# A two-block transformer kernel on one core: the expert layers' tokens scattered to expert regions, expert weights kept in SBUF, and the middle of the kernel put in a written order

## The chip, the core and the metric

The kernel runs on one core of a Trainium2 chip. The metric is the device time of one execution in microseconds; the median of 3 runs of the kernel before is 853.11 us (852.16 to 854.4). All arithmetic is in fp32. PE is the matmul engine (PEld its weight load), DVE the vector engine, ACT the activation engine, POOL the general engine, which also issues the indirect DMAs, and SP the engine that issues the plain DMAs.

## The reference, cut to what matters

The input x has 16 sequences of 128 tokens with 128 features. Every layer adds to x what it computes from a normalized x:

```python
x = x + xcond(ln(x), cond, ctx)       # self-attention, cross-attention to ctx, GLU feed-forward
x = x + ffn0(ln(x))                   # shared gated expert + 7 routed gated experts, top 2
x = x + slots(cond, ctx, ln(x))       # 3 turns of slot attention over ctx
x = x + ffn1(ln(x))                   # 8 routed experts (relu), top 1
```

The two expert layers, which the change is about:

```python
def expert(h, g, u, d):               # g, u: 352 x 128, d: 128 x 352
    return einsum('...i,hi->...h', silu(h @ g.T) * (h @ u.T), d)
# ffn0: 2048 tokens
out = expert(x, sg, su, sd)           # shared, for every token
probs = softmax(x @ wr.T + rb); scores, idx = top_k(probs, 2); scores /= scores.sum()
out += sum over the 2 chosen e of scores[e] * expert(x, rg[e], ru[e], rd[e])
# ffn1: 2048 tokens
p = softmax(x @ w_gate + b_gate); e = argmax(p)
out = (relu(x @ W1[e] + b1[e]) @ W2[e] + b2[e]) * max(p)    # W1: 128 x 512, W2: 512 x 128
```

## The kernel before, in words

Tokens lie 128 to a batch on the partitions; r (128 x 16 x 128) holds the running sum of all 16 batches. After attention the work is done in four groups of four batches (512 tokens).

The order of work is set in two ways. The two attention phases stand in a `manual_schedule` block (lines 798 to 802): each engine gets its instructions in the order in which the code issues them. All the rest is put in order by the framework's scheduler, by priority (the order of the code) and its own estimate of when things are ready; on the chip each engine then works through its queue in order.

1. Loads on SP (lines 114 to 131), self-attention and cross-attention (to about 408 us). The softmax shares of cross-attention go into tiles "es" with four buffers (line 459).
2. GLU feed-forward: `glu_norm` and `glu_prologue` normalize a group on DVE, transpose it on PE and scale it on DVE (line 544). `glu_body` takes four columns, each of two 128x512 matmuls, a Gelu on ACT and a product on DVE, and then the output matmuls. `wide` tiles in PSUM have three buffers.
3. First expert layer. `moe0_route` normalizes a group (`Routed.normed`, scaled on DVE by `scale_shift`, line 230), computes the routing logits, marks the two best experts (`one_hot_max`, called twice), and writes tokens and weight to a table `tok` in DRAM. When all groups are routed, `Routed.sort` gives each token-expert pair a place in a list sorted by expert (line 940 on), inverts that list by masks on DVE and small matmuls on PE (lines 983 to 1009), and so finds for each tile of 128 places which rows to fetch (`frm`) and where results go (`to`). `moe0_shared` computes the shared expert for each group. `silu_gate` writes silu as a Tanh on ACT and two scalar_tensor_tensor steps on DVE.
4. `Routed.tiles` runs the 38 tiles (lists of different experts don't share a tile, hence 38 for 4096 pairs). Per tile: `fetch` gathers 128 rows by an indirect DMA on POOL (line 1054); `weights` reads the expert's row into a register on SP and loads 576 KB of weights from DRAM (line 1044, six buffers); a transpose, 6 up-matmuls, the gate, 3 down-matmuls, a scale on ACT (line 1173), and an indirect DMA on POOL that scatters the results to `res0` in DRAM (line 1075). `combine` reads `res0` back and adds.
5. `slot_prologue` prepares the slot layer's weights and `slot_context` its keys and values from ctx; it adds a row to all 16 rows of "cb" on one partition, on POOL (line 1232). `slot_turns` runs the 3 turns, the groups one step apart.
6. Second expert layer: `moe1_route`, `sort`, and 23 tiles, as before with one expert per token. The sort of this layer also issues matmuls that compute nothing needed (`busy`, line 975).

The steps that the code itself does not name: `ln_stats` takes statistics by bn_stats on DVE, and the root by a `pow` on POOL (line 177); `t_tag(g)` are four PSUM tiles, one for each group; `value_load` (line 1041) is a register load.

## Time and profile before

| | us |
|---|---|
| median of 3 runs | 853.11 |
| the profiled execution, its own time | 857.12 |
| its span, first to last instruction | 855.4 |
| attention ends (last "ya" on PE) | 407.8 |
| first up-matmul of the first expert tiles | 502.75 |
| last scale of a first-layer tile | 590.9 |
| last r of the slot turns | 772.6 |
| last up-matmuls of the second layer's tiles begin | 847.9 |

The busy totals and the 40 slices of the page, each slice 21.4 us:

```profile
PE 783.4 (92%) x5415; PEld 615.5 (72%) x5415; DVE 575.8 (67%) x1820; ACT 431.7 (50%) x940; POOL 350.5 (41%) x440
...
PE   6999999999999999999899889989858989995987
...
PEclk9999999999999999999999989999889979985899
DMA  8200000001100000000200169974100000003893
```

A digit is a tenth of the slice in which the engine was busy; PEclk is the granted clock in tenths of full speed; DMA is the mean busy share of 16 DMA engines. The two stretches with a DMA digit of 9 are the tiles of the two expert layers. The rows that cost most on the engines which the change touches (count, then busy us and mean ns, then idle time before them):

```profile
L1158 PE MATMUL gum<-zTnm,wm 128*128 128x128 f32 x456 | 63.6, 282 | 0.0
L1054 POOL DMA_INDIRECT zsm<-tok,frmm x38 | 36.8, 968 | 32.5 <-DVE secm L1032 21.2
L1075 POOL DMA_INDIRECT res<-ysm,tom x38 | 37.3, 982 | 17.5 <-ACT ysm L1173 9.0
L1135 DVE SCALAR_TENSOR_TENSOR gsm<-thm,gum 128x384 f32<-128x384 f32 x38 | 21.1, 554 | 26.8 <-ACT thm L1133 26.1
```

In names of tiles the layer's letter is appended: m for the first expert layer, n for the second. An fp32 matmul shows as two records, so the 456 of the first row are 228 matmuls: six for each of 38 tiles. Since records of matmuls overlap, the rate of PE is read from the chain of work, where 12 such passes take 1.34 us.

### The profile page before, as it was taken

The numbers are of one execution on the slowest core, as the hardware profiler recorded it, in microseconds if no ns is written. First come the engines' busy times: TensorE is split into PE (matmuls) and PEld (weight loads), VectorE is DVE, ScalarE is ACT, GpSimd is POOL, SyncE is SP. The second block draws the span as 40 slices with busy tenths as digits, with TensorE's granted clock in tenths as the row PEclk, the third lists the DMA queues.
The fourth block names the chain that finished last, engine by engine and source line by source line (L and its number), as shares of the span: only waits on it lengthen the run. The fifth ranks groups of instructions, "written<-read, shape, count | busy, mean of one in ns | idle before, by whom it ended". The sixth has DMA issues, their size and how long they took to land.

```text
span 855.4 us, 15453 instructions
## 1 busy us (share of the span) xinstructions
PE 783.4 (92%) x5415; PEld 615.5 (72%) x5415; DVE 575.8 (67%) x1820; ACT 431.7 (50%) x940; POOL 350.5 (41%) x440
## 2 busy tenths in 40 slices
PE   6999999999999999999899889989858989995987
PEld 4688888877788777776656579988446756664876
DVE  3677768665856777797788946554477758867444
ACT  3567667676654554445122124434467757851332
POOL 2234233323233333436522077773443324432776
PEclk9999999999999999999999989999889979985899
DMA  8200000001100000000200169974100000003893
GB/s 312 98 2 1 2 1 2 1 2 41 38 25 11 11 11 11 11 11 1 79 26 26 59 217 324 334 261 143 51 1 2 1 1 1 13 25 117 312 333 132
DMA packets 36528, 65.18 MB, mean 76 GB/s; under 512 B 4578, under 2 KB 25013, under 8 KB 35811
## 3 DMA queue, kind: packets, MB, share of 16 engines
q1 hardware_dynamic: 32179, 55.11, 19.2%
q0 software_dynamic: 4272, 9.09, 3.4%
q8 instruction: 43, 0.70, 0.3%
q14 instruction: 34, 0.28, 0.1%
HBM read 55.71 MB, written 8.93 MB: 76 GB/s over the span
## 4 chain that ended last, share of the span: by engine, by line
PE 64%; DVE 15%; DMA 8%; POOL 5%; issue 3%; ACT 3%; SPq 0%; POOLq 0%; ACTq 0%; DVEq 0%
PE pq L325 6%; PE gum L1158 4%; PE pk L335 4%; PE te L482 4%; PE po L492 4%; PE s L429 4%; PE s L420 3%; PE ya L524 3%; PE pv L342 3%; PE pv L358 3%; PE ya L515 3%; DMA zsm<-tok,frmm 2%; PE ynm L1169 2%; DMA res<-ysm,tom 2%; PE glu L838 2%
## 5 line engine op out<-in xcount | busy, mean ns | idle before, releaser
L467 POOL TENSOR_TENSOR e<-e,ri 128x1024 f32<-128x1024 f32 x32 | 61.1, 1909 | 143.5 <-DVE ri L453 130.4
L440 DVE TENSOR_REDUCE mx<-s 128x8 f32<-128x1024 f32 (+1 forms) x64 | 64.4, 1006 | 63.2 <-PE s L429 47.7
L452 DVE TENSOR_REDUCE ri<-e 128x8 f32<-128x1024 f32 (+1 forms) x64 | 63.7, 995 | 18.9 <-ACT e L448 18.2
L461 POOL TENSOR_TENSOR es<-e,ri 128x512 f32<-128x512 f32 x64 | 43.4, 706 | 67.0 <-DVE ri L453 32.5
L325 PE MATMUL pq<-ha,wa 128*128 128x256 f32 x256 | 67.1, 398 | 2.7 <-ACT q L326 1.7
L445 DVE TENSOR_TENSOR e<-s,mx 128x1024 f32<-128x1024 f32 (+1 forms) x64 | 63.8, 997 | 2.0
L1158 PE MATMUL gum<-zTnm,wm 128*128 128x128 f32 x456 | 63.6, 282 | 0.0
L448 ACT ACTIVATE e<-e 128x1024 f32<-128x1024 f32 (+1 forms) x64 | 57.1, 892 | 5.9 <-DVE e L445 4.0
L1158 PEld LDWEIGHTS gum<-zTnm,wm 128*128 128x128 f32 x456 | 59.2, 199 | 0.1
L325 PEld LDWEIGHTS pq<-ha,wa 128*128 128x128 f32 x256 | 46.7, 199 | 10.4 <-ACT q L326 3.1
L1054 POOL DMA_INDIRECT zsm<-tok,frmm x38 | 36.8, 968 | 32.5 <-DVE secm L1032 21.2
L1075 POOL DMA_INDIRECT res<-ysm,tom x38 | 37.3, 982 | 17.5 <-ACT ysm L1173 9.0
L335 PE MATMUL pk<-ctxT,wa 128*128 128x154 f32 x256 | 40.5, 295 | 0.6 <-ACT k L336 0.6
L482 PE MATMUL te<-ident,e 128*128 128x128 f32 x256 | 39.6, 277 | 0.0
L482 PEld LDWEIGHTS te<-ident,e 128*128 128x128 f32 x256 | 30.5, 141 | 12.1 <-issue 8.7
L1135 DVE SCALAR_TENSOR_TENSOR gsm<-thm,gum 128x384 f32<-128x384 f32 x38 | 21.1, 554 | 26.8 <-ACT thm L1133 26.1
L429 PEld LDWEIGHTS s<-k,q 64*128 64x128 f32 x512 | 31.4, 190 | 10.4 <-issue 9.6
L483 ACT COPY eT<-te 128x512 f32<-128x512 f32 x64 | 37.8, 591 | 0.0
L496 ACT COPY oT<-po 128x512 f32<-128x512 f32 x32 | 18.5, 578 | 36.0 <-PE po L492 36.0
L420 PE MATMUL s<-k,ha 128*128 128x308 f32 x128 | 36.1, 423 | 0.0
L429 PE MATMUL s<-k,q 64*128 64x128 f32 x512 | 34.5, 281 | 1.8 <-DVE e L445 1.8
L335 PEld LDWEIGHTS pk<-ctxT,wa 128*128 128x128 f32 x256 | 35.1, 190 | 1.0 <-ACT k L336 0.9
(410 smaller groups left out, 2035.6 us busy)
## 6 DMA issues: line engine op xcount, KB each, us to landing
wm<-in_moe_w_dram SPq DMA_DIRECT2D x38, 576.0 KB
wn<-in_moe_w_dram SPq DMA_DIRECT2D x23, 578.0 KB
wa<-in_attn_w_dram SPq DMA_DIRECT2D x4, 1024.0 KB
ygm<-res SPq DMA_DIRECT2D x8, 256.0 KB
vor<-vo SPq DMA_DIRECT2D x16, 104.0 KB
vr<-vor SPq DMA_DIRECT2D x8, 208.0 KB
tok<-stm SPq DMA_DIRECT2D x4, 258.0 KB
tok<-stn SPq DMA_DIRECT2D x4, 258.0 KB
```

Of the source, the lines that this page charges most:

```text
L325: PE.matmul(pq[:, j, :], lhsT=wqk[:, w : w + P], rhs=hT, start=True, stop=True)
L335: PE.matmul(pq[:, j, :], lhsT=wqk[:, w : w + D], rhs=kvT, start=True, stop=True)
L420: PE.matmul(ps[:, par, : 4 * nk].rearrange("p (j k) -> p j k", k=nk), lhsT=st["qT"][:, i * P : (i + 1) * P], rhs=st["kT"][:, h0 : h0 + 4, ...
L429: PE.matmul(ps[:, par, j * nk : (j + 1) * nk], lhsT=st["qT"][h0 : h0 + DH, c, i * P : (i + 1) * P], rhs=st["kT"][h0 : h0 + DH, c, i * nk : ...
L440: V.tensor_reduce(self.mx, self.ps, AX.X, ALU.max)
L445: V.tensor_tensor(self.e, self.ps, self.mx.unsqueeze(3).to_broadcast([P, 2, 4, nk]), ALU.subtract)
L448: S.activation(self.e, self.e, AF.Exp, scale=1.0 / math.sqrt(DH))
L452: V.tensor_reduce(self.ri, self.e, AX.X, ALU.add)
L461: G.tensor_tensor(t[:, 8 * k0 : 8 * k1].rearrange("p (h k) -> p h k", h=8), e[:, :, k0:k1], ri.to_broadcast([P, 8, k1 - k0]), ALU.mult,)
L467: G.tensor_tensor(self.e, self.e, self.ri.unsqueeze(3).to_broadcast([P, 2, 4, self.nk]), ALU.mult)
L482: PE.transpose(t[:nk, j, :], e[:, par, j, :], ident)
L1158: PE.matmul(ps[j][:, c * P : (c + 1) * P], lhsT=w[:, k : k + P], rhs=zT, start=True, stop=True)
```

## The change

- **Scatter in place of sort and gather.** DRAM holds for each expert a region of 2048 rows (`disp`), filled once at the start with empty rows whose last word says that they belong to no token. As soon as a group is routed, `rank` counts its tokens' places in their experts' regions, and `send` scatters each batch by an indirect DMA on POOL, once for each of the two choices: 32 scatters in the first layer, 16 in the second. Each row carries features, weight and, as its last word, where its result goes. `plan` only finds where each tile starts. A tile's rows are then one plain DMA on SP (`fetch`, register load on SP, 8 buffers, 6 ahead), and its result is scattered by the row numbers in the tile itself, with empty rows dropped.
- **Weights kept in SBUF.** `load` brings all experts' weights into one tile (`wall`) by 7 or 8 DMAs. `weights` copies a tile's part from there, at an offset in a register: 768 or 516 columns on DVE, 384 or 640 on ACT, three buffers each.
- **Norms on ACT.** `act_scale` takes the place of `normalize` and `scale_shift` for GLU groups 2 and 3, the routed groups, and the contexts; the scaling of `hg` is on ACT too for those GLU groups.
- **Silu as one step.** ACT computes Silu, and DVE one product.
- **Written order.** From the GLU of group 1 to the loads of the second layer's weights, and around the second layer's tiles, a `manual_schedule` block gives the order. The slot prologue's pieces are dealt out over the tiles, one to a tile from the fifth on. Down-matmuls follow two tiles behind, transposes go two tiles ahead.
- "cb" lies on four partitions, so that its row addition is 128x512; "es" has three buffers; the `busy` matmuls of the sort are gone with it.

The core of the diff:

```diff
+    def dispatch(nm, ne, nt, pairs, w, k):
+        rows_ = -(-(ne * NTOK + (nt * P - pairs)) // (P * 4)) * P * 4
+        t = dram.tile([rows_, w], F32, name=f"disp{nm}")
...
+        V.memset(pad[:, :, w - 1 :].bitcast(I32), NONE)
+        n = rows_ // (P * k)
+        dma(
+            out=t.rearrange("(p n k) w -> p n (k w)", n=n, k=k),
+            in_=pad.rearrange("p k w -> p (k w)").unsqueeze(1).to_broadcast([P, n, k * w]),
+        )
...
-                t = self.ap_.tile([P, 8 * NC], F32, name=f"es{self.nm}", tag="es", bufs=4)
+                t = self.ap_.tile([P, 8 * NC], F32, name=f"es{self.nm}", tag="es", bufs=3)
...
+    def act_scale(z, src, rs, nmr):
+        for i in range(4):
+            S.activation(z[:, i, :], src[:, i, :], AF.Identity, bias=nmr[:, i : i + 1], scale=rs[:, i : i + 1])
...
+        def turned(self, i):
+            z = self.st[i][:, 0, :, :D]
+            t = transpose_n(z, P, 4, f"{self.nm}{i}", i)
+            self.zT[i] = rt.tile([P, 512], F32, name=f"zT{self.nm}{i}", tag="zT", bufs=4)
+            S.copy(self.zT[i], t.rearrange("p a b -> p (a b)"))
+            S.copy(self.st[i][:, 1, :, :D], z)
...
+        def rank(self, i):
...
+            PE.matmul(pr, lhsT=before, rhs=self.any[:, gs, :], start=True, stop=False)
+            PE.matmul(pr, lhsT=ones, rhs=self.cum[:, gs, :], start=False, stop=True)
...
+        def send(self, i):
+            for b in range(4):
+                for k in range(self.nk):
+                    G.indirect_dma_start(
+                        out=self.sent[(4 * i + b) * self.nk + k],
+                        out_offset=bass.IndirectOffsetOnAxis(ap=self.to[i][:, k, b : b + 1], axis=0),
+                        in_=self.st[i][:, k, b, :], in_offset=None,
+                    )
...
+        def address(self, part):
+            j = len(self.ws[part])
+            if j < self.nt:
+                self.at[part] = (V, S)[part].value_load(
+                    self.row[0:1, j : j + 1], min_val=0, max_val=(self.ne - 1) * self.wn
+                )
+
+        def weights(self, part):
...
+            (V.tensor_copy, S.copy)[part](w, self.wall[:, bass.ds(self.at[part] + part * self.up, n)])
+            self.ws[part].append(w)
+            self.address(part)
+
+        def fetch(self):
...
+            z = rt.tile([P, 2 * D + 2], F32, name=f"zs{self.nm}{j}", tag="zs", bufs=ZBUFS)[:, : self.width]
+            row = nc.sync.value_load(self.first[0:1, j : j + 1], min_val=0, max_val=self.disp.shape[0] - P)
+            dma(out=z, in_=self.disp[bass.ds(row, P), :])
...
             def finish(j):
...
+                down(self.ws[1][j], acts[j], y, ys, zs[j])
+                self.weights(1)
                 G.indirect_dma_start(
+                    out=wrote[j],
+                    out_offset=bass.IndirectOffsetOnAxis(ap=zs[j][:, self.width - 1 :].bitcast(I32), axis=0),
+                    in_=ys, in_offset=None, bounds_check=dst.shape[0] - 1, oob_is_err=False,
                 )
+                self.fetch()
...
+            for j in range(nt + 2):
+                if j + 2 < nt:
+                    turn(j + 2)
+                if j < nt:
+                    acts[j] = up(self.ws[0][j], zT[j], f"{self.nm}{j}", j)
+                    self.weights(0)
+                if j >= 2:
+                    finish(j - 2)
+                if j >= 4 and extras:
+                    extras.pop(0)()
...
     def silu_gate(a, gate, up, nm, n):
-        S.activation(th, gate, AF.Tanh, scale=0.5)
...
-        V.scalar_tensor_tensor(gs, th, 1.0, gate, ALU.add, ALU.mult)
-        V.scalar_tensor_tensor(a, gs, 0.5, up, ALU.mult, ALU.mult)
+        S.activation(gs, gate, AF.Silu)
+        V.tensor_tensor(a, gs, up, ALU.mult)
...
+    with tc.manual_schedule():
+        m0.stats(0)
+        glu_stats(2)
+        glu_c(1, 0)
+        m0.scale(0)
+        glu_c(1, 1)
+        m0.turned(0)
+        glu_c(1, 2)
+        route_first(m0, 0)
+        glu_z(2)
+        glu_c(1, 3)
+        glu_in(2)
+        glu_residual(2)
+        route_second(m0, 0)
+        glu_c(2, 0)
+        glu_y(1)
+        m0.stats(1)
+        glu_stats(3)
+        m0.send(0)
...
+        shared_steps((0, 1), (0, 2))
+        m0.scale(3)
+        shared_steps((1, 0))
+        m0.turned(3)
+        shared_steps((0, 3))
+        route_first(m0, 3)
+        shared_steps((1, 1))
+        route_second(m0, 3)
+        m0.send(3)
+        shared_steps((1, 2))
+        m0.plan()
+        shared_steps((2, 0), (1, 3), (2, 1), (2, 2), (3, 0), (2, 3), (3, 1), (3, 2), (3, 3))
+        m0.tiles(moe0_up, moe0_down, slot_prologue())
+        for g in range(4):
+            m0.results(g)
+        for g in range(4):
+            if g > 1:
+                m0.combine(g - 2)
+            slot_context(g)
+        for g in (2, 3):
+            m0.combine(g)
+        m1.load()
+    slot_turns(range(4), lambda g: m0.sum[g])
...
     for g in range(4):
         moe1_route(m1, g)
-    m1.sort()
-    m1.tiles(moe1_up, moe1_down)
+    for g in range(4):
+        m1.send(g)
+    m1.plan()
+    with tc.manual_schedule():
+        m1.tiles(moe1_up, moe1_down)
```

`plan` also issues the first three register loads and copies of each part, and the first six fetches. In the written order, groups 1 and 2 follow the pattern of group 0, with the columns of the next GLU group or of the shared expert between the steps of the routing.

## The prediction, made before the change was run

> **What bounds the kernel now.** I read the busy time in stretches that I cut at the stages, because the page's shares average stages with different limits (columns: busy us and instruction count of PE, PEld, DVE, ACT, POOL; granted clock; DMA share; GB/s).
> ```profile
> 412.00:450.00 38.00, 34.16 (x165) 21.62 (x165) 33.33 (x141) 9.86 (x17) 17.04 (x34) 1.00 0.18 59
> 450.00:475.00 25.00, 24.29 (x122) 15.58 (x121) 20.98 (x93) 5.71 (x12) 3.84 (x10) 1.00 0.07 22
> 475.00:502.00 27.00, 21.51 (x116) 14.26 (x115) 20.60 (x81) 2.77 (x6) 9.60 (x10) 0.86 0.45 154
> 502.00:592.00 90.00, 86.28 (x734) 85.02 (x733) 50.09 (x116) 39.04 (x116) 64.00 (x67) 0.96 0.77 260
> 612.00:757.00 145.00, 120.05 (x675) 89.17 (x676) 107.53 (x542) 103.97 (x268) 58.47 (x100) 0.91 0.02 5
> 757.00:794.00 37.00, 27.29 (x122) 20.02 (x120) 23.45 (x153) 8.75 (x22) 9.26 (x17) 0.60 0.28 82
> 794.00:856.00 62.00, 52.32 (x390) 47.88 (x390) 28.71 (x92) 20.39 (x69) 42.84 (x44) 0.94 0.75 264
> ```
> PE is busy in 502 to 592 and nearly so in 412 to 475; 475 to 502 and 757 to 794 are the sorts, where it starves and the clock sags (0.86, 0.60). The chain in order of time says what stands there.
> ```profile
> 419.88 5.26 DVE stm L230 x4
> ...
> 489.66 1.23 POOL zsm L1054
> ...
> 493.70 6.31 DMA zsm<-tok,frmm
> ...
> 531.79 5.01 DMA zsm<-tok,frmm
> ...
> 539.49 4.95 DMA res<-ysm,tom
> ```
> From 463.8 to 489.5 it is DVE alone (sort, L1007 masks, silu), then gathers; inside the tiles only a patch at 531 to 566 is DMA. The 419.88 line is explained by the instructions of that window:
> ```profile
> 419.80 4.49 POOL L1232 TENSOR_TENSOR cb<-cb,brow 1x2048 f32<-1x2048 f32 x1
> 419.88 5.01 DVE L230 TENSOR_SCALAR stm<-r,ym,mvm 128x128 f32<-128x128 f32 x3 [1.04 <-POOL mvm L201]
> ```
> A norm of 0.26 us sat through a 4.5 us POOL operation.
>
> **Part by part.** Durations are of the profiled execution: span 855.4, own time 857.1, 4.0 above the median of 853.1. I sum differences and take them off the median.
>
> *Start and attention: 0 (-1 to +3).* The fills write 15,360 rows of 520 B and 17,408 of 1,032 B, 26 MB; at the 260 GB/s of the tile stretch, 100 us, queued on SP behind the loads at 16 us. Cover: that queue's next user, the stores of L404, starts at 199.5. The memsets on DVE (0.1 to 0.3 us) precede the first x at 2.9. Three "es" buffers: the transposes that free one (L503, 347.3) lead the write into it (L461, 352.1) by 4.8 us, so nothing.
>
> *Middle, 411.4 (last yg of group 0) to the first tile at 502.* PE work by the chain: GLU columns 12 x 1.72 us (two matmuls of 0.86) = 20.7, GLU outputs 3 x 3.6, transposes 4.7, router 3.5, ranks 2, shared columns 12 x 1.72 = 20.7, shared outputs 4 x 2.6: 73. Removed from DVE: scale (L230, 9.4), zgl and hg of two groups (5), context norms (4.9), one of two silu steps (12 x 0.68), the masks of the sort (12): it falls from 75 to about 42 us, ranks included. ACT rises from 18 to some 40. POOL gets 32 scatters; a DMA_INDIRECT lasts 0.94 and they come 1.25 apart (L1054), 40 us, plus six norms of 1.8 and residuals, under 60 in all. None exceeds PE, so what costs is the written order: an in-order engine that waits holds what is behind it. Walking it: scale(0) needs the norm chain (0.7 add, 0.9 stats, 0.5, POOL 1.4, ACT 1.7 = 5.2 us), and the GELUs behind it on ACT hold their PSUM: PE waits about 1.9 us; rank(0) waits 2.1 for DVE's one-hots; z(3) and hg(3) cost 3; rank(3) 1.3: 8.3. The plan puts three register loads and three copies each on DVE and ACT; ACT's first load waits for the row that DVE works out (some 3 us of 0.17 us steps), and the silu of shared column (2,0) is queued behind it: 6 us, of which PE has 4.5 to do (two matmuls, an output): 1.5. With 1.5 for table loads (below), the tiles start at 411.4 + 73 + 11.3 = 495.7: -6.5 (-13 to 0). The last sends begin at some 474, end 10 us later, land by 486.5, the first fetch by 489: under shared work. SP's waits for the sends hold later fetches alone, and those PE needs only from 495.
>
> Silu may need another table than Tanh. The trace of before shows Gelu, Tanh, Gelu (430.86, 431.57, 432.64) with no load between; a load lasts 1.28 (L670) and the next ACTIVATE follows at once. Written order changes Silu/Tanh five times: 0 to 6.4 us of ACT. The Trainium skill (ScalarE: Activation LUTs, "What ACT_TABLE_LOAD costs") says a switch is 1.28 plus a drain of 1.38: 13 us. By the row, a quarter of 6.4 reaches PE, as three PSUM tiles run ahead: 1.5; by the rule 3. I take the row.
>
> *First tiles, 38.* PE's part is unchanged: 12 passes up twice 0.67, 0.67 down, 0.11 turn = 2.12 us. Gone: 22 MB of weight loads and 38 gathers, with the 8 us patch. New per tile on DVE: a copy of 768 columns; 128x208 took 0.256 (L392) and 128x32 0.166, hence 0.54; plus a product of 0.55 in place of two. On ACT: copy 384 (0.48, between 0.27 for 128 and 0.59 for 512), silu 0.50, turn 0.27, scale 0.37 = 1.6. Both also load a register: on SP that takes 0.27 + 0.15 + 0.02 = 0.44 (L1041); hidden behind their own copies, or else DVE is 1.55 and ACT 2.05, just below 2.12. POOL falls from two DMAs to one, 1.25. Here a rule speaks against the change: the skill (SBUF — State Buffer, the "DVE blocks DMA" trap) says an fp32 copy in SBUF locks POOL out of writing descriptors. The trace shows the lock between compute (4.5 us above), but three norms of that kind ran at 500.22 in 0.85 us beside a gather of 0.94, its usual time. By the row, scatters cost 1.25; by the rule 1.25 + 0.54 = 1.8, still covered. Steps total 38 x 2.12 - 1.3 (no down in the first two) + 1.4 (the last two) = 80.7; the prologue's sixteen pieces add 3 of PE and four norms of 1.6 on ACT, stalls of 2. That is 86 us against 88.1 (first up 502.75, last scale 590.9): -2 (-6 to +8).
>
> *Hand-over: -1.5 (-5 to +2).* Before, 13 us from the last scale to slot start. Still there: last scatter (at least 2.2 to land), reads, combine. Contexts 0 and 1, about 4.5 each in order, fill the wait: 11.5.
>
> *Slots: +1 (-2 to +4).* Same instructions; contexts 2 and 3 now run into the first turns.
>
> *Last layer: +3 (-5 to +9).* Before, from the last r at 772.6: first tile 794.2, steady from 800.3, last up at 847.9. The sort's twelve us on DVE go. But sixteen scatters x 1.25 = 20 us enter POOL's queue. Before, group 0's one-hot came only at 769.1 and its weight at 772.6 (L1388, L1399), at the end of the slots, so I let the sends start at 773, with two POOL norms of 1.5 between: 796; landing 2.4, fetch 2.4, turn: 801.5. Behind these sends nothing waits on POOL but those norms; PE waits for all of it, and the busy matmuls that kept it warm are gone. 23 tiles at 2.17 follow: DVE has copy 0.41, two relus 0.6, two sums 0.63, ACT 1.7, register load 0.44 each: tight, +1. The 4 us stall at 818 to 833 goes. Up(22) then comes at 849.3 plus 1, before 847.9, and the two late downs add half a microsecond: +3. If groups 0 to 2 send during the slots: -5.
>
> Sum: -6.5 - 2 - 1.5 + 1 + 3 = -6. 857.1 becomes 851; on the median **847**.
>
> **Rivals.**
> *Everything overlaps (832).* Middle stalls 5 instead of 11 (-6), no tile stalls (-2), early sends in the last layer (-7, part of their 8): 847 - 15. For it: POOL was 9.3 busy of 37 there; against: low-priority route steps came late before.
>
> *No change (853).* The last layer's queue and ACT's register loads eat the gain: first tiles at 2.2 (+3), last layer at its +6 (+3): 847 + 6. For: ACT at 2.05 of 2.12; against: register loads have copies to hide behind.
>
> *Slower (868): the ring of eight fetched tiles.* A buffer is refilled only when its tile's scatter, which reads its row numbers, has landed. From turn to end of down is 10.6 us (five steps), then scale 0.5, POOL 0.2, scatter, fetch: 11.4 + both landings, for eight tiles of 17.0. It decides from landings of 5.6 together. The page shows scatters 2.2 least, 4.6 median; gathers 2.4 and 5.2. At the least, 16.0: free. At the medians, 21.2, 2.65 per tile: +20 and +11, less some 10 of stalls counted above that fall into the same waits: 847 + 21. Against: those medians were beside weight loads of 260 GB/s that go; a tile now moves 130 KB in 2.1 us.
>
> That the change doesn't do what it says can't be: the loads, scatters and copies are instructions.
>
> **How the numbers follow.** A measurement here tells 0.3% (2.6 us) from nothing. Likeliest (847; own range 840 to 852) 0.47; overlap 0.22; no change 0.14; ring 0.17. Of the first, 0.04 lies above 850.5: faster 0.65, same 0.17, slower 0.18. The range goes from 830, below the overlap case, to 860, part of the way to the ring.
>
> **What would show it.** First up-matmul of the tiles near 496 (before 502.75), PE clock 1.0 throughout; masks and gathers absent; a step of 2.12 between turns, ACT under 2.1; table loads on ACT where Silu meets Tanh; the wait before the fetch on SP names the scatter if the ring binds; POOL's sends in a row from 773 to 796 in the last layer with PE idle and a low clock behind. I am wrong if attention stretches under the fills, if the written order stalls PE over 15 us, or if the slots change length.

## The result, and the profile after

The changed kernel takes 902.17 us (900.47 to 903.9, four runs) beside 853.75 for the kernel before in the same rounds: 1.0569 times as long (95% interval 1.0537 to 1.0601). The forecast was 847, a little faster. The profiled execution took 903.62 at a span of 901.9 and a mean clock of 0.935 (before: 857.12, 855.4, 0.951).

The page after, to set beside the busy totals and the 40 slices of before (a slice is now 22.5 us):

```profile
PE 784.0 (87%) x5367; PEld 613.4 (68%) x5367; DVE 550.1 (61%) x1700; ACT 481.5 (53%) x1058; POOL 335.3 (37%) x430
...
PEclk9999999999999999998988999799969899975998
DMA  8999700001200000006000111023500000003220
```

PE is busy for as long as before, to 0.6 us; the two stretches of DMA 9 in the tiles are gone, as they should be, and the fills stand in slices 2 to 4, where they cost nothing: group 0's output matmuls begin at 407.4 (before 407.6). DVE has 26 us less, ACT 50 more. So the 46.5 us by which the span grew are time in which PE waits. Busy time by stage, after (columns: stretch, its length, busy us and count of PE, PEld, DVE, ACT, POOL, granted clock, DMA share, GB/s):

```profile
411.40:520.70 109.30, 84.79 (x361) 52.81 (x360) 54.24 (x209) 35.16 (x74) 46.77 (x65) 0.88 0.21 71
520.70:621.00 100.30, 88.91 (x743) 87.50 (x744) 45.16 (x115) 57.38 (x166) 44.49 (x55) 0.95 0.15 43
621.00:800.10 179.10, 154.01 (x819) 108.87 (x817) 124.06 (x624) 116.85 (x295) 67.58 (x116) 0.90 0.11 39
800.10:831.00 30.90, 7.26 (x30) 5.93 (x30) 11.97 (x88) 8.07 (x18) 19.22 (x22) 0.52 0.25 86
831.00:884.80 53.80, 46.47 (x357) 43.26 (x357) 32.55 (x102) 29.48 (x84) 18.32 (x19) 0.96 0.23 65
884.80:901.90 17.10, 4.22 (x34) 3.70 (x32) 3.19 (x10) 1.30 (x4) 4.29 (x5) 0.76 0.03 9
```

Three stages of before, cut at the same events (the middle, the gated tiles, the last layer's first to last up-matmul):

```profile
411.40:502.60 91.20, 81.16 (x401) 51.95 (x400) 76.10 (x316) 19.06 (x35) 31.36 (x54) 0.96 0.23 76
502.60:590.90 88.30, 85.12 (x730) 84.24 (x728) 49.38 (x112) 38.26 (x114) 63.12 (x65) 0.97 0.78 264
794.20:847.10 52.90, 49.09 (x366) 45.02 (x366) 26.17 (x84) 19.63 (x66) 39.40 (x40) 0.96 0.88 307
```

The events that cut the stages are the first up-matmul of the gated tiles, the last scale, the end of the last r of the slots, and the first and last up-matmul of the second layer. The forecast counts from the times of the chain (502.75 and 847.9 in the table of before); the timeline has these two matmuls at 502.6 and 847.1. In us:

| stage | before | after | difference | forecast |
|---|---|---|---|---|
| attention, to 411.4 | 411.4 | 411.4 | 0 | 0 |
| middle | 91.2 | 109.3 | +18.1 | -6.5 |
| 38 gated tiles | 88.3 | 100.3 | +12.0 | -2 |
| hand-over and slots | 181.7 | 179.1 | -2.6 | -0.5 |
| head of the last layer | 21.6 | 30.9 | +9.3 | +7 |
| its first to last up | 52.9 | 53.8 | +0.9 | -5 |
| its end | 8.3 | 17.1 | +8.8 | +0.5 |

**The middle.** PE is busy 84.8 us and idle 24.5. In the stretches at half clock it is busy 23.7 us. If all of that work ran at half speed, half of it, 11.8, is the clock's loss, and 84.8 less 11.8 leaves 73.0, the work that was forecast. The waits before each rank and the half clock behind them are what was missing. The longest, in the timeline of after (start, us, engine, line, in brackets the idle time before and what ended it):

```profile
486.44 0.96 POOL L1006 DMA_INDIRECT dispm<-stm,tom  x1 [0.30 <-issue]
...
488.84 0.17 DVE L962 COPY stn<-idx 128x4 int32<-128x4 int32 x1 [7.93 <-DMA dispm<-stm,tom]
...
488.92 0.68 DVE L1192 TENSOR_TENSOR r<-ym,r 128x512 f32<-128x512 f32 x1
...
492.95 0.60 PE L991 MATMUL rankm<-anym,before 128*128 128x28 f32 x2 [7.17 <-DVE anym L1161]
```

The copy of row numbers at 488.84 belongs to the *second* expert layer. It stands outside the written block; the scheduler had room for it early and put it into DVE's queue, and as the staging buffers of both layers share a tag of three, it waits for the last scatter of gated group 2 to land. DVE works in order: r, the one-hots and rank(3) stand behind it. What such a wait does to PE's clock shows when the stretch around it is cut:

```profile
485.80:490.80 5.00, 0.00 (x0) 0.00 (x0) 1.79 (x9) 0.00 (x0) 1.29 (x2) 1.00 0.08 27
490.80:497.60 6.80, 4.65 (x10) 2.58 (x10) 3.47 (x19) 0.80 (x2) 1.91 (x2) 0.50 0.03 10
497.60:502.30 4.70, 4.70 (x32) 3.74 (x31) 3.83 (x22) 0.00 (x0) 3.50 (x4) 1.00 0.18 58
```

Of the other five waits of 2.25 us or more in this stage, four have 3.4 or 6.8 us at 0.50 behind them; the fifth, 2.68 us at the plan, does not. The changes of the clock lie on a grid of 3.41 us, and in this stage they go with how busy PE was in one such window. Two windows that the half clock follows, and the two that share the plan's wait:

```profile
412.30:415.71 3.41, 1.16 (x3) 0.14 (x1) 3.07 (x17) 0.88 (x3) 2.50 (x7) 1.00 0.73 209
470.33:473.74 3.41, 1.40 (x6) 1.01 (x7) 2.77 (x16) 0.20 (x1) 0.00 (x0) 1.00 0.03 11
501.05:504.46 3.41, 2.14 (x14) 1.31 (x12) 1.69 (x6) 1.02 (x2) 2.50 (x4) 1.00 0.12 39
504.46:507.87 3.41, 2.00 (x5) 1.04 (x6) 2.19 (x5) 1.60 (x3) 0.70 (x1) 1.00 0.15 44
```

The Trainium skill (TensorE: Matmul & The Clock Gate, "Part 1: The HAM clock gate") says that the clock is halved after an idle window of about 3.4 us, the window running free. The length and the grid agree with this trace. The idle window need not be whole here: PE was busy 1.16 and 1.40 us of the two that the half clock follows, and 2.00 and 2.14 us left it at 1.00 (ends of matmuls are modelled, so these figures are near ones).

**The gated tiles.** They run at 2.12 us each, as forecast, except from 557 to 583, where the four context norms stand among them:

```profile
564.18 0.86 DVE L203 BATCH_NORM_STATS2 stc<-ctxn 77x6 f32<-77x128 f32 x4
...
565.70 1.04 POOL L193 TENSOR_TENSOR yc<-qqc,mhalf 77x4 f32<-77x4 f32 x1
566.82 0.20 POOL L217 TENSOR_TENSOR mvc<-mvc,yc 77x4 f32<-77x4 f32 x1
567.05 1.65 ACT L868 ACTIVATE ctxn<-ctxn,mvc,yc 77x128 f32<-77x128 f32 x4 [3.27 <-POOL mvc L217]
568.60 0.24 ACT L1099 COPY zTnm<-tnm 128x128 f32<-128x128 f32 x1
568.75 0.48 ACT L1173 ACTIVATE gsm<-gum 128x384 f32<-128x384 f32 x1
569.26 0.55 DVE L1174 TENSOR_TENSOR am<-gsm,gum 128x384 f32<-128x384 f32 x1 [3.64 <-ACT gsm L1173]
...
570.28 0.86 DVE L203 BATCH_NORM_STATS2 stc<-ctxn 77x6 f32<-77x128 f32 x4
```

ACT waits 3.3 us for POOL's root, the tile's silu stands behind the norm on ACT, the tile's product behind it on DVE, and the next statistics behind the product: a circle of 6.1 us for a step of 2.12.

**The last layer's tiles** have a circle of their own. One step:

```profile
858.81 0.73 ACT L1075 COPY w1n<-walln 128x640 f32 x1 [1.18 <-DVE ysn L1483]
...
859.85 0.63 ACT L1474 ACTIVATE an<-h1n,w0n 128x128 f32<-128x128 f32 x2
...
860.52 0.43 DVE L1075 COPY w0n<-walln 128x516 f32 x1 [0.89 <-ACT an L1474]
861.28 0.29 DVE L1483 TENSOR_TENSOR ysn<-ynn,w1n 128x128 f32<-128x128 f32 x1 [0.34 <-PE h1n L1469]
...
861.66 0.73 ACT L1075 COPY w1n<-walln 128x640 f32 x1 [1.18 <-DVE ysn L1483]
```

The code refills the weight buffer that the current tile has just read. ACT's relu reads its bias there, so DVE's copy waits for the relu; DVE's bias sum reads the other, so ACT's copy waits for the sum; and the next relu stands behind that copy. The circle turns in 2.6 to 2.85 us with neither engine full.

**The end.** After the last landing (893.3), for 8 us, nothing runs but a closing DRAIN on POOL, which began at 890.9. The rows of the last source line, after and then before (durations least, median and most in ns):

```profile
L1680 POOLq DRAIN  x3: 45/113/10198, 890.9 to 901.6; - x3
```
```profile
L1569 POOLq DRAIN  x3: 45/107/3068, 851.5 to 855.1; - x3
```

### The profile page after: what moved, and what is told of

It is laid out like the page before. It is cut to its first block, busy times and chain, and to the rows that moved or that the text cites. A ratio compares the mean times of both kernels' runs of the same rounds, so it can differ in the third digit from the quotient of the medians.

```text
span 901.9 us, 15855 instructions
## 1 busy us (share of the span) xinstructions
PE 784.0 (87%) x5367; PEld 613.4 (68%) x5367; DVE 550.1 (61%) x1700; ACT 481.5 (53%) x1058; POOL 335.3 (37%) x430
## 4 chain that ended last, share of the span: by engine, by line
PE 64%; DVE 10%; POOL 9%; issue 8%; ACT 5%; DMA 2%; POOLq 0%; SPq 0%; ACTq 0%; DVEq 0%
PE pq L341 6%; PE gum L1199 5%; PE s L436 3%; PE pk L351 3%; PE s L445 3%; PE po L508 3%; PE pv L374 3%; PE te L498 3%; PE ya L540 3%; PE pv L358 3%; PE ya L531 3%; PE ynm L1206 3%; POOL out_dram L1106 2%; PE glu L886 2%; PE gu L1184 2%
## 5 line engine op out<-in xcount | busy, mean ns | idle before, releaser
L477 POOL TENSOR_TENSOR es<-e,ri 128x512 f32<-128x512 f32 x64 | 43.3, 704 | 70.5 <-DVE ri L469 30.7
L1106 POOL DMA_INDIRECT res<-ysm,zsm x38 | 37.7, 992 | 69.7 <-ACT ysm L1209 69.6
L1199 PE MATMUL gum<-zTnm,w0m 128*128 128x128 f32 x456 | 60.0, 284 | 0.0
L1199 PEld LDWEIGHTS gum<-zTnm,w0m 128*128 128x128 f32 x456 | 57.3, 202 | 0.0
L341 PEld LDWEIGHTS pq<-ha,wa 128*128 128x128 f32 x256 | 46.5, 199 | 10.5 <-ACT q L342 3.0
L1174 DVE TENSOR_TENSOR am<-gsm,gum 128x384 f32<-128x384 f32 x38 | 21.0, 554 | 51.9 <-PE gum L1199 35.0
L1206 PE MATMUL ynm<-w1m,am 128*128 128x128 f32 x228 | 33.9, 287 | 11.4 <-ACT ysm L1209 11.4
L1106 POOL DMA_INDIRECT out_dram<-ysn,zsn x23 | 22.6, 983 | 44.1 <-DVE ysn L1484 44.1
L1206 PEld LDWEIGHTS ynm<-w1m,am 128*128 128x128 f32 x228 | 29.9, 200 | 12.6 <-ACT ysm L1209 12.6
L1006 POOL DMA_INDIRECT dispm<-stm,tom x32 | 31.1, 973 | 17.4 <-issue 9.1
```

Of the source, the lines that this page charges most:

```text
L341: PE.matmul(pq[:, j, :], lhsT=wqk[:, w : w + P], rhs=hT, start=True, stop=True)
L1106: G.indirect_dma_start(out=wrote[j], out_offset=bass.IndirectOffsetOnAxis(ap=zs[j][:, self.width - 1 :].bitcast(I32), axis=0), in_=ys, in_ ...
L1199: PE.matmul(ps[j][:, c * P : (c + 1) * P], lhsT=w[:, k : k + P], rhs=zT, start=True, stop=True)
L1206: PE.matmul(y, lhsT=a[:, c * P : (c + 1) * P], rhs=w[:, c * D : (c + 1) * D], start=(c == 0), stop=(c == 2))
```

## The experiments

The runs fell on chips of two sorts, which has to be known to read them: on some the kernel before takes 852 to 856 (the result above, e5 to e8, e16 to e18), on others 899 to 902. Its time in the same rounds stands in the table, with the stages of each profile as cut above (the time of the first gated up-matmul, then lengths, all in us). e1 to e4 ran on one chip, e5 to e8 on another, e9 to e12, e13 to e15, e16 and e17, and e18 likewise. The edits are shortened to what matters.

| run | kernel before | this | ratio (interval) | first up | tiles | slots | head | first to last up | end |
|---|---|---|---|---|---|---|---|---|---|
| e1 | 901.7 | 909.5 | 1.014 (1.008-1.020) | 524.5 | 102.2 | 177.3 | 30.8 | 54.6 | 17.1 |
| e2 | 901.7 | 893.6 | 0.995 (0.992-0.998) | 523.3 | 87.7 | 178.1 | 30.8 | 54.0 | 17.1 |
| e3 | 901.7 | 897.1 | 0.997 (0.993-1.001) | 523.6 | 100.3 | 179.2 | 31.0 | 45.8 | 17.1 |
| e4 | 901.7 | 916.0 | 1.020 (1.013-1.026) | 526.4 | 99.3 | 199.6 | 19.1 | 54.2 | 17.1 |
| e5 | 852.7 | 852.4 | 1.000 (0.997-1.003) | 501.1 | 87.4 | 178.8 | 21.6 | 51.4 | 8.4 |
| e6 | 852.7 | 898.3 | 1.054 (1.050-1.057) | 515.5 | 102.3 | 177.0 | 31.2 | 53.8 | 17.1 |
| e7 | 852.7 | 880.3 | 1.032 (1.028-1.037) | 518.7 | 88.2 | 175.6 | 30.7 | 47.1 | 17.1 |
| e8 | 852.7 | 911.9 | 1.068 (1.063-1.073) | 525.0 | 103.9 | 179.2 | 30.7 | 54.1 | 17.1 |
| e9 | 899.4 | 906.8 | 1.008 (1.005-1.011) | 523.7 | 100.3 | 179.2 | 30.9 | 53.9 | 17.1 |
| e10 | 899.4 | 907.2 | 1.009 (1.005-1.012) | 524.3 | 102.2 | 183.8 | 26.1 | 54.2 | 17.1 |
| e11 | 899.4 | 883.7 | 0.982 (0.976-0.989) | 520.1 | 88.3 | 177.0 | 30.7 | 44.7 | 17.1 |
| e12 | 899.4 | 880.1 | 0.979 (0.972-0.985) | 519.0 | 89.8 | 180.8 | 26.1 | 43.8 | 17.1 |
| e13 | 898.7 | 897.9 | 0.999 (0.996-1.002) | 510.6 | 106.4 | 181.2 | 21.6 | 72.4 | 8.3 |
| e14 | 898.7 | 872.1 | 0.970 (0.963-0.976) | 506.1 | 89.9 | 178.1 | 31.2 | 46.5 | 17.1 |
| e15 | 898.7 | 869.9 | 0.967 (0.960-0.973) | 506.7 | 89.3 | 177.0 | 31.1 | 44.1 | 17.1 |
| e16 | 856.5 | 875.2 | one run | 508.9 | 101.4 | 175.7 | 19.9 | 54.5 | 13.2 |
| e17 | 856.5 | 901.7 | one run | 519.8 | 100.1 | 178.1 | 31.0 | 53.9 | 17.1 |
| e18 | 854.0 | 854.4 | 0.999 (0.995-1.003) | 491.1 | 89.3 | 178.2 | 31.6 | 44.6 | 17.1 |

**e1, the second layer's row numbers tied to the last r.**

```diff
-V.tensor_copy(at, rows_)                       # second layer
+V.tensor_scalar(none, r[:, 4 * i + 3, 0:1], 0.0, None, ALU.mult)
+V.tensor_scalar(at, rows_, none, None, ALU.add)
```


> The copies of row numbers into the staging buffers of the last layer are tied to the last value of r, so that they can't stand in DVE's queue among the routing of the gated layer; all else as in the changed kernel (902). Theory A (a copy for the last layer, at 488.84, waits for a scatter of the gated layer and holds DVE, and with it rank(3) on PE, from 481 to 489): PE's wait of 7.2 us before rank(3) goes, the first tile's up-matmul moves from 520.9 to about 512, and the time falls by 8 (5 to 12) to 894. Rival B (the wait is only the first of several: the sends, the plan and the first fetch stand behind it and take its place): first up-matmul within 3 us of 520.9, time 899 to 902.

The copy is gone from the middle, but the first up-matmul is not earlier: 524.5, where e2 and e3, which keep the copy, have 523.3 and 523.6 on the same chip. PE still waits 6.3 us before rank(3) (7.2 in e2 and e3), now for another reason: on this chip results of PE reach ACT and DVE late. PE and ACT in the timeline of e1:

```profile
485.38 1.96 PE L1188 MATMUL gu<-zTm,wsh 128*128 128x512 f32 x4
...
490.27 0.60 ACT L1177 ACTIVATE gss<-gu 128x512 f32<-128x512 f32 x1 [7.07 <-remote]
```

The silu needs only the first of the matmuls of 485.38 and starts 3.9 us after it; DVE, which waits for the matmuls before, starts at 490.22, within 0.05 us of ACT, so it is PE's result that is late and not one of the two readers. Such delays show on all three chips of this sort (not in every run), and on none of the others. Rival B has the number, but e1 doesn't decide what the copy alone costs.

**e2, each context norm cut in two extras.**

```diff
-[partial(context_norm, g) for g in range(4)]
+[partial(f, g) for gs in ((0, 1), (2, 3)) for f in (context_stats, context_scale) for g in gs]
```


> The four context norms among the tiles are cut in two extras each (statistics one or two steps ahead of the scale), nothing else. Theory A (each norm was one round trip DVE statistics, POOL mean and power, ACT scale inside one step, 5.85 us for a step of 2.12, four times, 15 us): the stall from 557 to 583 goes but for 2 or 3 us, the tile stage falls from 100.1 to about 88, the time by 12 (8 to 15) to 890. Rival B (the stall comes from POOL, which issues scatters in the same queue, or from the weight copies, and would stand with any extras): at most 3 us less, 899 to 902.

```profile
523.30:610.90 87.60, 83.62 (x743) 82.59 (x743) 44.81 (x115) 57.25 (x166) 44.71 (x55) 1.00 0.17 49
```

The tiles take 87.6 us with the same instructions, and the clock stands at 1.00. Theory A holds: the circle was all of the 12 us.

**e3, refill one step later, last layer only.**

```diff
+if late and j: self.weights(0)      # the buffer of tile j - 1
 acts[j] = up(self.ws[0][j], zT[j], f"{self.nm}{j}", j)
-self.weights(0)                     # the same for weights(1) and down
```


> In the last layer alone a weight buffer is refilled one step after its last reader (of three buffers, the one freed by the tile before), ahead of this tile's own work, instead of right behind its last reader. Theory A (the step of 2.58 us is a circle: ACT's relu reads the bias in w0, so DVE's copy into that buffer waits for it; DVE's bias sum reads w1, so ACT's copy waits for that, and the next relu stands behind it): a step of 2.2, 20 steps, time down by 8 (6 to 9) to 894. Rival B (the copies and register loads themselves fill DVE and ACT: 1.67 and 1.62 us of work a step, and 0.5 each for the register): 2.5 or more a step, 900 to 902.

From the first to the last up-matmul it is 45.8 us, 2.08 a step, 8 us less. Theory A holds: the copies themselves fit into a step.

**e4, route and send each group right behind its slots.**

```diff
 slot_close(it, g, kept[g])
+if it == T_SLOTS - 1: moe1_route(m1, g); m1.send(g)    # gate1 made before the slots
```


> The gate's matrix of the last layer is worked out before the slots, and each group is routed and sent right behind the end of its own slots instead of after those of all groups. Theory A (the head of the last layer is POOL's queue of 16 sends, 1.25 us apart, from 802 to 826): twelve sends go out before the last group's slots end, the first up-matmul comes 18 to 22 us after the last r instead of 30.7, and the time falls by 8 (4 to 12) to 894. Rival B (POOL's powers and ACT's norms of the other groups' slots wait behind the sends, so that the slots get longer by what the head gets shorter): 898 to 904, with the last r some 8 us later.

The head falls to 19.1, as theory A has it, and the slots grow by 20 (199.6 beside 179.2 in e3 on the same chip). In the chain, norms of the slots stand on POOL behind four sends each (at 788.2 and 823.0). Rival B holds, at more than its price.

**e5, the kernel before.**

> The kernel before, unchanged, as a reference on the chip of these runs. If the changed kernel's loss is its own, this one takes 853 (850 to 857), some 5.5% less than the changed kernel in the same rounds; if it was a matter of the chip, the two come within 1%.

The time is as expected, and the stages are near those of the first profile.

**e6, the middle left to the scheduler's order.** The written block begins at the plan instead of at the first norm.

> The middle, from the first norm of the gated layer to the last send, is left to the scheduler's order by priority; the plan, the last shared columns and the tiles keep the written order. Theory A (what costs the middle is the order written out: PE, in order, stands before each rank and each norm's transpose, and its clock drops to 0.5 for some 5 us behind each stand; before, with a scheduler's order, PE was at 1.00 all through 412 to 486): first up-matmul at about 504 instead of 521 to 523, time 884 (880 to 890). Rival B (the chains of routing themselves, DVE one-hots, rank, index, sixteen microseconds of sends on POOL, are as long in any order): first up-matmul at 515 to 523, time 896 to 902.

The first up-matmul comes at 515.5, which is rival B's number. PE is idle 22.1 us and loses 6.9 to the clock. So the first up-matmul says that the scheduler's order cures little. It doesn't say why: the last layer's row numbers stand in DVE's queue here three times, and each time wait 4 to 5 us for a landing of the sends. Two of the three:

```profile
481.23 0.17 DVE L962 COPY stn<-idx 128x4 int32<-128x4 int32 x1 [5.02 <-DMA dispm<-stm,tom]
500.14 0.17 DVE L962 COPY stn<-idx 128x4 int32<-128x4 int32 x1 [5.36 <-DMA dispm<-stm,tom]
```

The waits of PE right behind the three copies (3.3, 3.4 and 4.2 us) are 10.9 of the 22.1 us. So e6 tests the scheduler's order and these copies together; e18 shows that the waits are not the work's own.

**e7, e2 and e3 together.**

> The split context norms and the later refill of the last layer's weight buffers together. Theory A (two stalls in two stages, nothing shared): their gains of 8 and 4.6 add, 889 (886 to 892). Rival B (the clock gives back in one stage what is won in the other, as the spread between runs hints): 892 to 896.

The two stages keep their gains (88.2 and 47.1, where e6 on the same chip has 102.3 and 53.8). The 889 of theory A was summed from a chip of the other sort and can't be held against 880.3. Against the first 902.2, on a chip of the same sort, 21.9 us are won, and 18.8 of them lie in these two stages: the clock took nothing back, against rival B.

**e8, Silu back to two steps.**

```diff
-S.activation(gs, gate, AF.Silu)
-V.tensor_tensor(a, gs, up, ALU.mult)
+S.activation(gs, gate, AF.Tanh, scale=0.5)
+V.scalar_tensor_tensor(gs, gs, 1.0, gate, ALU.add, ALU.mult)
+V.scalar_tensor_tensor(a, gs, 0.5, up, ALU.mult, ALU.mult)
```


> Silu is taken back to its two-step form (Tanh on ACT, two products on DVE) in the changed kernel; all else stays. Theory A (one ACT_TABLE_LOAD is all that Silu brings and PE covers DVE's second product in the tiles, 0.55 us of 2.12): no difference, 899 to 905. Rival B (DVE with its weight copy of 0.55 and register load has no room for a second product: 0.55 x 38 and more round trips): 912 or more. Rival C (Silu's table load stalls the middle): 896 or less.

It is slower: 1.068 against the 1.057 of the changed kernel. The tiles start at 525.0 (518.7 in e7, which has the unchanged middle on the same chip) and take 103.9 (102.3 in e6). Rival B has the number but not the place: on this chip most of the loss is in the middle, and DVE is busy only 66 of 104 us of the tiles. That the second product costs where DVE is a link in a chain of waits is the likely reading, not shown. Silu as one step is a gain of some 9 us within the change.

**e9, the changed kernel again.**

> The changed kernel, unchanged, as the reference for the runs beside it. 902 (899 to 905), a ratio of 1.057 to the kernel before, with its stages as in the first profile: first up-matmul at 520.7, tiles 100, slots 179, first tile of the last layer 31 behind the last r, 71 from there to the end.

Time and stages are within 5 us of those of the first profile, the ratio is not: here the kernel before takes 899.4. e13 tells why.

**e10, row numbers as in e1; gate's matrix before the slots, a group's sends behind its routing.**

```diff
 for g in range(4):
     moe1_route(m1, g)
-for g in range(4):
     m1.send(g)
```


> Two parts in two stages that don't touch. The last layer's row numbers are again tied to the last r, this time beside a reference on the same chip; and in the last layer the gate's matrix is worked out before the slots and a group's four sends stand in the program behind its own routing, not behind that of all four groups; the routing itself keeps its place behind the slots. Theory A: PE's wait before rank(3) falls from 7.2 to 3 or less and the first up-matmul comes at about 513 to 516; the head of the last layer shrinks from 31 to about 25, slots unchanged; 902 - 6 - 6 = 890. Rival B: rank(3) waits for its one-hots all the same (first up at 519 to 522) and POOL's sends stay in a row behind the last r (head 30 to 31): 899 to 904.

The wait before rank(3) falls from 7.2 (e9) to 5.6 us and no more; again this is a chip with late results of PE. The head is 4.8 shorter, as theory A has it, but the slots are 4.6 longer. Nothing is won: 907.2 beside 906.8 in e9.

**e11, the ranks later, on top of e7.**

```diff
-R.rank(i)                  # in route_second
+place(m0, i)               # rank and weights: behind glu_y(1), glu_c(3, 2), shared (0, 2), (1, 3)
```


> On top of the split norms and the later refill (880 on another chip), each rank matmul of the gated layer moves two GLU or shared columns further back in PE's order (rank(0): behind GLU output 1), with its sends, so that DVE's one-hots are done when PE comes to it. Theory A (of 109 us of the middle PE is idle 24.5, 16 of it before the four ranks, and loses 11.8 to half clock behind these waits; its work is 73): idle falls to some 12, the clock's loss to 4, first up-matmul at 502 to 508, time 866 (862 to 871). Rival B (the waits only move on: to the sends, the first fetch, or the plan, as the free order's did): first up at 514 to 519, time 876 to 881.

Rival B holds: no wait before a rank is left, but PE now waits 4.3 us behind DVE's statistics, 3.6 for an output's last product, and 5.9 behind the plan, while ACT does its register loads and copies. The first up-matmul moves only from 523.7 (e9) to 520.1.

**e12, all mends so far.**

> All mends together: split norms, later refill, later ranks, row numbers tied to the last r, gate's matrix early and sends behind their own group. Theory A: 866 from the later ranks, 3 from the row numbers, 6 from the head of the last layer, 857 (850 to 863), level with the kernel before or up to 1% above it. Rival B (the sends of the last layer and the waits of the middle stay): 870 to 880.

It takes 880.1, the upper end of rival B; head and slots trade as in e10.

**e13, the kernel before with the bounds check on its gated scatters.**

```diff
-**({} if self.nk == 2 else dict(bounds_check=NTOK - 1, oob_is_err=False))
+bounds_check=dst.shape[0] - 1, oob_is_err=False
```


> The kernel before with one thing added: the scatters of its gated layer's tiles carry the bounds check that those of the changed kernel carry (no row is out of bounds here, so none is dropped). Theory A (POOL's closing DRAIN grows with the number of checked scatters, 61 instead of 23): DRAIN 10 instead of 3.1, time up by 7, ratio 1.008. Rival B (it grows with rows dropped, of which this adds none, or with something else): DRAIN 3.1, time within 0.3%.

The DRAIN is 3.07 us and the time the same, so it is not the checks. This also is the profile of the kernel before (but for the check) on a chip where it takes 900. Its gated tiles, and its last layer from first to last up:

```profile
510.60:617.00 106.40, 92.75 (x728) 89.69 (x728) 49.83 (x112) 37.65 (x114) 60.24 (x61) 0.93 0.67 216
...
819.80:892.20 72.40, 55.15 (x367) 50.58 (x367) 25.90 (x84) 19.57 (x66) 39.62 (x40) 0.88 0.69 224
```

The same tiles took 88.3 and 52.9 us at 264 and 307 GB/s on the first chip. Some 38 of the 45 us between the chips lie in these two stages, where weights are loaded from DRAM; the changed kernel, which loads them once, differs by 5 (902.2 and 906.8).

**e14, a new written order of the middle.** The same steps, each placed behind enough PE work to cover what it waits for; with e1's row numbers, e2 and e3. The beginning:

```python
m0.stats(0); glu_stats(2); glu_c(1, 0); glu_c(1, 1); m0.scale(0); glu_c(1, 2); glu_z(2); glu_stats(3); glu_c(1, 3)
m0.turned(0); glu_residual(2); glu_in(2); glu_z(3); route_first(m0, 0); route_second(m0, 0); glu_y(1); m0.stats(1)
glu_c(2, 0); glu_c(2, 1); glu_in(3); place(m0, 0); glu_residual(3); glu_c(2, 2); glu_c(2, 3); glu_c(3, 0); m0.send(0)
```


> Split norms, later refill, row numbers tied to the last r, and a new written order of the middle, the same steps and no other work: every step that PE waits for is written three or more PE steps behind what it needs (the scale of a group two columns behind its statistics, its transpose two more, the rank behind the next outputs, the plan last but one). Theory A (the order sets the middle, the work being 73 us of PE): PE idle 5 to 10 instead of 24.5, half clock under 3, first up-matmul at 490 to 498, time 853 to 860 on a chip where the kernel before takes 853. Rival B (POOL's 32 sends, each behind its own group's chain, and DVE's and ACT's turns set it): first up at 508 to 516, time 870 to 878.

The first up-matmul comes at 506.1, between the two forecasts. Two waits of 3.7 and 3.9 us are of the kind that e1 showed, so the run leaves open what is the chip's.

**e15, e14 with row numbers of their own for the padding rows, and so no check on the gated scatters.**

```diff
+dma(out=t.rearrange("(p n) w -> p n w", n=n)[:, :, w - 1 :].bitcast(I32), in_=own.unsqueeze(2))
```


> The run before with one more part: the padding rows of the gated layer get row numbers of their own behind the result's rows, so that its 38 scatters need no bounds check and drop nothing (one more fill of 15,360 numbers of 4 bytes at the start). Theory A (checks or drops make the closing DRAIN long): DRAIN 3 instead of 10.2, 7 less than the run with the new order alone, below the kernel before by 0.3 to 1% if the new order does what it should. Rival B (DRAIN 10 all the same, or 768 more rows written cost the scatters time): the same as the new order alone within 0.3%.

The DRAIN is 10.20, so it is not the rows dropped in the gated layer either (the last layer's 23 scatters still carry the check).

**e16, no sends.**

> The changed kernel without its 48 sends: the routing is worked out, but no row goes to the experts' regions, so that all tiles hold padding and the results stay at the zeros that two more fills at the start write. Theory A (the sends make the closing DRAIN long): DRAIN 3 instead of 10.2. Rival B (something else does): 10.2. Of the sends' price: if POOL's queue is what the last layer's head waits for, its first up-matmul comes 10 to 14 us behind the last r instead of 31; if the waits of the middle come from routing and not from the sends, the first up-matmul of the gated tiles stays within 6 us of 521.

The DRAIN is 6.26, between the theories. 109 indirect DMAs gave 10.20 and 61 give 6.26, which is 0.082 us for each of the 48 sends. The kernel before has 122 and 3.07, so the count alone is not the rule. The head is 19.9: of the 31.0 us in e17 on the same chip the sends are 11. PE's waits in the middle, in the timeline:

```profile
467.57 0.38 PE L992 MATMUL rankm<-anym,before 128*128 128x28 f32 x2 [2.36 <-DVE anym L1162]
483.51 0.38 PE L992 MATMUL rankm<-anym,before 128*128 128x28 f32 x2 [2.36 <-DVE anym L1162]
```

Without a landing to wait for, rank(3) waits 2.4 us like the others, where e17 on the same chip has 7.2. The middle is 10.9 us shorter than there. The other waits of the written order remain, and 18.7 us of idle time.

**e17, scatters of the tiles led by a fixed table** (`ap=own[:, j : j + 1]` in place of the fetched tile's column).

> The changed kernel with the tiles' scatters led by a fixed table of row numbers in place of the column of the fetched tile, so that results land in other rows than they should. Theory A (row numbers read from a fetched, strided tile make the DRAIN long): DRAIN 3 instead of 10.2. Rival B: 10.2, and the same time as the changed kernel within 3 us.

The DRAIN is 10.20 and the time the old one, so it is not the place of the row numbers.

**e18, the kernel of e15 again.**

> The kernel of the new order with unchecked scatters, once more, unchanged. On a chip where the kernel before takes 853: Theory A (the two long waits were that chip's own, PE delivering late): first up-matmul at 498 to 503 instead of 506.7, time 860 (855 to 865), a ratio of 1.00 to 1.015, that is, the middle is mended but the head of the last layer (31 us) and the closing DRAIN (10) still keep it from winning. Rival B (the order itself leaves them): 506 and 868. On a chip where the kernel before takes 900: 870 and 506 again, a ratio of 0.967.

```profile
411.40:491.10 79.70, 71.32 (x360) 47.14 (x360) 53.63 (x206) 35.14 (x74) 46.41 (x63) 0.98 0.28 93
491.10:580.50 89.40, 85.72 (x744) 84.39 (x743) 44.55 (x114) 57.35 (x167) 44.43 (x55) 0.98 0.19 54
```

The middle takes 79.7 us with the same steps that took 109.3, better than theory A. PE is idle 8.4, of which the longest wait, 3.7, is for the first fetched tile; the half clock behind it costs 2.3, of which 0.6 falls into this stage. So the work and the 32 sends, which are all still there, did not set the middle's time: the written order did, together with the place of the last layer's row numbers. e18 changes both, and no run on a chip of this sort parts them; e6, where the copies bring half of PE's idle time, says that their share need not be small.

The kernel is level with the one before where that takes 854, and 3.3% faster where that takes 899 (e15). Beside the first profile of before, e18 wins 11.5 us in the middle, 3.6 in hand-over and slots and 8.3 in the last layer's tiles, and loses 1.1 in the gated tiles, 10.0 in the head and 8.8 at the end.

## Why the prediction was wrong

The forecast was 52.5 us off (46.5 more, where 6 less were forecast). Three steps of it failed. The waits of the middle got 11.3 us and measured 36.3, half clock included. The norms among the gated tiles were priced by their work on ACT, where each held a circle of three engines for 6.1 us. In the last layer the circle of refills and the closing DRAIN stand in no term. The terms, one by one:

- *Start and attention, 0*: right. The fills are over at about 100 us.
- *"PE work by the chain ... 73"*: right to about 2 us. The profile after gives 73.0 (84.8 less 11.8), e18, with hardly any half clock in this stage, 70.7; the agreement to 0.1 is in part luck.
- *DVE "falls from 75 to about 42 us"*: 54.2 measured. It stayed under PE, but the waits of the four ranks for DVE's one-hots are 16.1 of the 24.5 us.
- *"-6.5"* is counted from 502; from the 502.75 of the table the same sum gives -7.
- *"Walking it: scale(0) ... 8.3"*: the walk found the waits that it looked at and sized those to about a microsecond (1.9 against 2.3 measured; z(3) and hg(3) 3 against 2.6; plan 1.5 against 2.7). It gave rank(0) 2.1 (3.1 measured), and rank(1) and rank(2) nothing (3.5 and 2.4), though each has the same chain of one-hots as rank(0); and rank(3) 1.3 (7.2). This last excess was not in the written order: the scheduler had put a copy of another layer into DVE's queue. e16 (7.2 to 2.4 without a landing) supports this; the clean test, e1, met a chip with late results of PE. In sum the waits are 24.5 for 11.3.
- *"PE clock 1.0 throughout"*: 11.8 us lost. The prediction read the sag to 0.86 and 0.60 in the profile of before and did not price it for its own eleven microseconds of waits.
- *Table loads, 1.5 by the row, 3 by the rule of the Trainium skill (ScalarE: Activation LUTs, "What ACT_TABLE_LOAD costs")*: both too much. In the whole middle there is one ACT_TABLE_LOAD, 1.28 us at 464.83; from then on Tanh and Silu alternate without any. The number of switches was wrong. Of the two prices the row's fits: the next ACTIVATE starts at 466.12, 1.3 us after the copy before the load has ended.
- *Tiles, "extras add 3 of PE and four norms of 1.6 on ACT, stalls of 2"*: the step that failed in this stage. The norms were costed as work on ACT; they were a circle through three in-order engines, 6.1 us each. All else of the 86 holds: e2 gives 87.6. The skill's trap (SBUF — State Buffer, "DVE blocks DMA") was hardly put to the test: most of the gated tiles' scatters ran between DVE's fp32 weight copies and lasted 0.96 to 0.99 us. The six that overlapped one by 0.3 us or more lasted 1.07 to 1.18.
- *Hand-over and slots*: right in sum (-2.6 for -0.5).
- *Last layer, +3*: the head was right (28.9 forecast, 30.9 measured; PE idle, clock 0.52), with sends as its largest part (11, e16). "23 tiles at 2.17 ... tight, +1" was costed as sums of busy time and missed the circle through the just-freed buffers, 2.45 a step on the mean; e3 gives 2.08. Of the end, +8.8, only half a microsecond is in a term: 7.1 of it is the closing DRAIN, which the profile of before shows only as 3 us in its last lines.
- *The rivals*: the ring of fetched tiles did not bind, since in e2 PE is busy 83.6 of the tiles' 87.6 us. The case that came, slower through waits that in-order engines hand on to each other, was named ("if the written order stalls PE over 15 us") and given no chance of its own.

On the chips that load fast, the removed loads were worth nothing in the gated tiles, where PE set the pace before and after (88.3, and 87.6 in e2), and some 4 to 8 us in the last layer once the later refill let them show (e7, e18). On the chips that load slowly they were worth some 17 us in the gated tiles and 26 to 28 in the last layer (e14 and e15 beside e13, on one chip). There the change has a gain, which the waits of in-order engines took at first; on the other sort even the kernel of e18 is only level, because the head and the end of the last layer take what its middle and its last tiles give.

**Still open**: what the closing DRAIN waits for (the sends add to it; the checks, the rows dropped in the gated layer and the place of the row numbers don't); why PE's results come late on some chips, which are those that load slowly; and how much of the middle's 29.6 us is the row numbers' and how much the order's, since a run of the scheduler's order with e1's row numbers, or of the old order with them on a chip without late results, is missing.

## What to carry to other kernels

When work of several engines is put in a written order, walk every wait of every queue, not a few, and price each twice: once as the wait, once as the half clock that can follow it (here 3.4 or 6.8 us at half speed). A piece of side work placed in a tight loop can cost its round trip through the engines (6.1 us here) and not its busy time (1.65 on ACT): issue its parts a step apart, and refill the buffer that was freed a step ago, not the one just read. An instruction of a later stage that shares a buffer tag can stand in the middle of an earlier one; look for names that don't belong.

## What the runs showed of the hardware

- After five of the six waits of PE of 2.25 us or more in the middle, the granted clock was 0.50 for one or two windows of 3.41 us; 24.5 us of waits cost 11.8 more. Windows of this grid in which PE was busy for 1.40 us or less were followed by the half clock; two with 2.00 and 2.14 were not.
- POOL's closing DRAIN took 10.20 us with 109 indirect DMAs (48 of them sends), 6.26 with 61 (no sends), and 3.07 to 3.13 in the kernel before with 122.
- The same program with weights streamed from DRAM took 853 us on some chips and 900 on others (264 and 216 GB/s in its gated tiles); with the weights kept in SBUF it took 902 and 907.
- Two DVE operations on fp32 tiles that else take 0.19 us lasted 0.96 and 0.92, until a 128x512 addition on POOL had ended (e11, 419.71 and 421.14); others that began under the same additions took their usual 0.18 to 0.19. POOL's scatters lasted 1.07 to 1.18 us where they overlapped a weight copy on DVE by 0.3 us or more, and 0.96 to 0.99 among the same tiles where they did not.
